# A masked-attention layer on one core: each output tile's scatter behind the next tile's adding gather, and one layernorm step moved behind the first natural tile

## The chip, the cores and the metric

The kernel runs on one core of one Trainium2 chip. The metric is the device time of one execution in microseconds (us); the kernel before takes 710.65 us, the median of 3 runs (710.3 to 715.59). The core has TensorE (PE), which multiplies; VectorE (DVE); ScalarE (ACT); GpSimd (POOL), which here mostly issues indirect DMAs; and SyncE (SP), which issues plain DMAs. Each works through its own queue in order. They meet at semaphores.

## What is computed

One layer of graph attention over 2708 nodes with 1024 features, with a layernorm ahead of it. The adjacency matrix holds a one with a chance of 0.0014771 at each place, so a node has some 4 neighbours.

```python
h = relu(layernorm(x))
q = h @ W_q.T + b_q;  k = h @ W_k.T + b_k;  v = h @ W_v.T + b_v
z = q @ k.T / sqrt(1024) * adj
z = where(z == 0, -10000, z)
x = x + relu(softmax(z, axis=1) @ v)
```

All tensors are float32.

## The kernel before

**Tiles.** The rows are cut into 22 tiles of 128 (21 full ones and a rest of 20). Since only neighbours count, no 2708 x 2708 matrix is formed. The product of the two weight matrices, M, is built first (`part_of_m`, L353, four parts on PE). Then, for every tile, q = h M + bias is formed on PE; the neighbours' rows of h are gathered one neighbour per row at a time (`gather`, L430) and multiplied with q on DVE for the scores (`scores`, L659); the weighted sum u of the same rows is formed on DVE (`sums`, L714); and u times W_v gives the output tile on PE.

**The opening.** `follow` (L239) works through strings of steps: `s14-15` loads the x rows of tiles 14 and 15 and takes their statistics on DVE (`stats`, L188), `r` takes the root of the variance on ACT and DVE (`root`, L209), `a` applies the layernorm (`apply`, L225), and `e9` loads a tile of the adjacency matrix and searches its rows for neighbours on DVE, with one pass on ACT (`edges`, L255). `apply` issues for each of its two tiles a relu on ACT (L233), a store of the rows to `h_dram` from POOL's queue (L234), and an addition into `hsum` on POOL (L235). ACT's order is that of the code here (a manual schedule); the other engines' order is set by a scheduler. After the four parts of M the first tile is turned (`turned`, L282) and multiplied (`query`, L298; L313), with the bias seeded into PSUM by ACT (L295). In the midst of that product `query` calls `open_first` for the first pair of tiles and then `follow(between[0])`. x rows lie in a ring of 7 row buffers, so that a load of later x rows or of h rows waits until an earlier holder is done with.

**Pairs of tiles.** After the first tile, tiles are taken in pairs (units). Five units hold tiles in natural order, five in an order sorted by number of neighbours (`sort`, L472, in the third unit), and ten are output units ("o"). `multiply` (L793) does a pair in seven block products instead of eight, from sums and differences of blocks (`blocks`, L518: a11, a12, a22, s1 to s4; s2 and s4 on POOL for the first units), four matmuls of 512 columns each to a block and two passes each in the profile. It calls `after(i)` between its steps. `after` moves the attention of other tiles on (`advance`, L770): gathers on POOL, scores and sums on DVE. From the sixth unit on DVE's order is that of the code too.

**The output of a tile.** In an output unit the results of a pair, ya and yb, are relued from PSUM by ACT (L866, L870, L874, L882), partly after an addition on DVE (L869, L873). L869 reads the PSUM bank into which PE adds its next block. Then POOL gathers the rows of x that belong to the tile and adds them in the DMA itself (`add_x`, L856, L859), and scatters the sum to `out` (`scatter`, L618, L619). `sent` holds the tiles whose scatter isn't issued yet; `send` issues them in `after(2)` and `after(5)`, and once behind the loop:

```python
def send(keep=0):
    while len(sent) > keep:
        y, t = sent.pop(0)
        scatter(y, t, P)
...
        def after(i):
            if i in (2, 5):
                send()
```

So ya, whose add is issued between `after(3)` and `after(4)`, is scattered at `after(5)` of the same unit, and yb at `after(2)` of the next one; each scatter waits for the landing of the add of its own tile. y tiles lie in four buffers. One tile is left over (`alone`, number 11 of the sorted order); it is done behind the loop, with its x rows gathered without an add (L1030), and so are the last 20 rows (`tail`, L895).

**The gathered rows.** 13 buffers of 0.5 MB hold gathered rows: `fill` (L644) issues a gather whenever one is free, and `sums` gives it back after its last use.

Of the kernel before, what the change touches and what calls it, by code (L numbers as in the profile page):

```python
# [15 lines left out]
ALU = mybir.AluOpType  # L16
AX = mybir.AxisListType

P = 128
# [4 lines left out]
SLOTS = 16  # L24
# [31 lines left out]
def tile_preln_masked_attention(  # L56
# [12 lines left out]
    nc = tc.nc  # L69
# [84 lines left out]
    t = 0  # L154
    while t < NT:
# [4 lines left out]
        t = e  # L160
# [7 lines left out]
    first = const.tile([P, PARTS, 8], FT, name="first")  # L168
# [70 lines left out]
    def follow(steps):  # L239

        for step in steps.split():
            if step == "a":
                apply()
            elif step == "r":
                root()
            else:

                with tc.issue_after(roots[-1].ins) if roots else nullcontext():
                    if step[0] == "s":
                        lo, hi = step[1:].split("-")  # L250
                        stats(range(int(lo), int(hi) + 1))
                    else:
                        adj_loads.append(edges(int(step[1:])))
# [44 lines left out]
    def query(hT, banks, name, first=False, between=(), mid=None):  # L298

        q = work.tile([P, D], FT, tag="q", name=f"q_{name}", bufs=4)  # L300
        order = [(h, c) for h in range(NH) for c in range(DC)]
        if first:

            order.sort(key=lambda hc: hc[1] >= DC // 2)
        def evict(h):
            nc.scalar.copy(q[:, h * NB:(h + 1) * NB], banks[h])

        for h, c in order:
            if mid is not None and (h, c) == (1, 5):
                evict(0)  # L310
                mid(mm)
                follow(between[0])
            mm = nc.tensor.matmul(banks[h], hT[:, c, :], M[:, c // 4, h, c % 4, :], start=False,  # L313
                                  stop=(c == DC - 1), skip_group_check=True)
        for h in range(NH) if mid is None else (1,):
            evict(h)
        follow(between[1])
        return q
# [4 lines left out]
    with tc.tile_pool(name="w", bufs=1, side="left") as wp:  # L323
# [74 lines left out]
        for t in range(2):  # L398
            h_e[t] = row_tile(f"h_e{t}")
            nc.sync.dma_start(h_e[t], h_dram[t * P:(t + 1) * P, :])  # L400
        follow("s14-15 e9 r e10 a")
        hT = {}

        def turn_first():
# [2 lines left out]
        banks = []  # L407
# [22 lines left out]
    def gather(dst, src, t, w, n, skip=False):  # L430
        off = bass.IndirectOffsetOnAxis(ap=ptab.bitcast(U32)[:n, t, w:w + 1], axis=0)
        if skip:
            return nc.gpsimd.indirect_dma_start(out=dst, out_offset=None, in_=src, in_offset=off,  # L433
                                                bounds_check=N - 1, oob_is_err=False)
        return nc.gpsimd.indirect_dma_start(out=dst, out_offset=None, in_=src, in_offset=off)
# [80 lines left out]
    behind = []  # L516
# [57 lines left out]
        ops_of[0][2]()  # L574
        banks_of[0] = banks_for(bp_sb)

    q = query(hT.pop(0), banks, "e0", first=True, between=('e11 s16-17', ''), mid=open_first)
    nc.scalar.dma_start(q_dram[0:P, :], q)

    steps_at = {(0, 0): 'e12 r a e13', (0, 3): 'e14 s18-19 r e15', (1, 0): 'a e16 s20-21 e17', (1, 3): 'e18 r a e19', (2, 0): 'e20 e21'}  # L580
# [37 lines left out]
    def scatter(y, t, n):  # L618
        to = nc.gpsimd.indirect_dma_start(  # L619
            out=out, out_offset=bass.IndirectOffsetOnAxis(ap=ptab.bitcast(U32)[:n, t, SLOTS:SLOTS + 1], axis=0),  # L620
            in_=y[:n], in_offset=None)
        for other in outs:
            tc.declare_no_dep(to.ins, other.ins, reason="rows of a permutation")
        outs.append(to)
# [231 lines left out]
    def add_x(y, t, n=P):  # L856

        off = bass.IndirectOffsetOnAxis(ap=ptab.bitcast(U32)[:n, t, SLOTS:SLOTS + 1], axis=0)
        nc.gpsimd.indirect_dma_start(out=y[:n], out_offset=None, in_=x, in_offset=off, compute_op=ALU.add)  # L859

    def o_results(ta, tb):
        ya = work.tile([P, D], FT, tag="q", name=f"y_{ta}", bufs=4)
        yb = work.tile([P, D], FT, tag="q", name=f"y_{tb}", bufs=4)

        def c11(X):
            nc.scalar.activation(ya[:, lo], X, AF.Relu)  # L866

        def c22(Y, p5):
            nc.vector.tensor_add(p5, Y, p5)  # L869
            nc.scalar.activation(yb[:, hi], p5, AF.Relu)  # L870

        def c12(Z, u2):
            nc.vector.tensor_add(u2, Z, u2)  # L873
            nc.scalar.activation(ya[:, hi], u2, AF.Relu)  # L874
            if ta == NT - 2:

                nc.sync.dma_start(tail_dram, ya[P - 1:, :])
            add_x(ya, ta)
            sent.append((ya, ta))

        def c21(Y):
            nc.scalar.activation(yb[:, lo], Y, AF.Relu)  # L882
            add_x(yb, tb)
            sent.append((yb, tb))

        return c11, c22, c12, c21

    sent = []

    def send(keep=0):  # L890
        while len(sent) > keep:
            y, t = sent.pop(0)
            scatter(y, t, P)

    def tail(t):  # L895
        n = tiles[t][1]
# [5 lines left out]
    def of_wv(i, j):  # L902

        return wv[j][:, i * 4:(i + 1) * 4, :]
# [4 lines left out]
    alone = order[-1]  # L909
# [30 lines left out]
    for n, unit in enumerate(units):  # L940
        kind, ta, tb = unit
        now[0] = n
        if n == FIRST:
            ordered.enter_context(tc.manual_schedule(engines={mybir.EngineType.DVE}))
        if FIRST - 1 <= n <= FIRST + 2:

            i, j = ((0, 0), (0, 1), (1, 0), (1, 1))[n - FIRST + 1]
            nc.sync.dma_start(m_dram[i, j], M[:, i, j])
        share = (20.0 if kind == "q" else 19.0) / 7
        nxt = units[n + 1] if n + 1 < len(units) else None  # L950
        results = (q_results if kind == "q" else o_results)(ta, tb)

        def after(i):
            if i in (2, 5):
                send()
            if (n, i) == (2, 3):
                with tc.issue_after(products[-1].ins):
                    placed.append(sort())
                ordered.close()
                ts_of_wv()  # L960
            if n == FIRST - 1 and i == 5:

                chain.append(behind[-1])
                next(stream)
            if n == FIRST - 1 and i == 6:
                chain.append(behind[-1])
            if (n, i) >= (FIRST, 0):
                advance(share)
            if nxt is not None:

                if i == (3 if n == FIRST - 1 else 0):
                    ops_of[n + 1] = blocks(*rows_of[n + 1], nc.gpsimd if n + 1 < FIRST - 1 else None)
                    ops_of[n + 1][1]()
                if i == (4 if n == FIRST - 1 else 2):
                    ops_of[n + 1][2]()
                    rows_of.pop(n + 1)
                    if n == last_q - 1:
                        all_rows()
                if i == 3:
                    banks_of[n + 1] = banks_for(bp_sb)  # L980
                if i == 2 and n + 2 < FIRST:
                    natural_rows(n + 2)
                if i == 4 and n + 2 >= FIRST and n + 2 < len(units) and n + 2 not in rows_of:
                    while units[n + 2][0] == "o" and not done.issuperset(units[n + 2][1:]):
                        advance(1.0)
                    rows_of[n + 2] = load_rows(units[n + 2])
            if (n, i) in steps_at:
                follow(steps_at[n, i])
            if (n, i) == (2, 1):
                searched()  # L990
            if n == last_q - 1 and i == 4:

                nc.sync.dma_start(bp_sb, bv.to_broadcast([P, D]))
                nc.vector.tensor_sub(bp_sb[:, NB:], bp_sb[:, NB:], bp_sb[:, :NB])

            for k, at in enumerate(((0, 0), (0, 1), (0, 3), (0, 4), (0, 5), (0, 6), (1, 2))):
                if (n - last_q, i) == at:
                    place, src = ((M[:, 0, 0], of_wv(0, 0)), (T[:, 0], tv_dram[0]), (T[:, 1], tv_dram[1]),
                                  (M[:, 1, 0], of_wv(1, 0)), (M[:, 1, 1], of_wv(1, 1)), (T[:, 2], tv_dram[2]),
                                  (T[:, 3], tv_dram[3]))[k]  # L1000
                    nc.sync.dma_start(place, src)

        multiply(n, results, after)
    ordered.close()
    send()
    while alone not in done:
        advance(1.0)

# [18 lines left out]
    nc.vector.tensor_copy(flag, ps_f[:, 0:1])  # L1027

    y = work.tile([P, D], FT, tag="q", name="y_alone", bufs=4)
    gather(y, x, alone, SLOTS, P)  # L1030
    tail(NT - 1)
    r, = load_rows(("o", alone))
    uT = turned(r, "alone")
# [16 lines left out]
    with tc.If(some > 0):  # L1050
        with tc.tile_pool(name="big", bufs=1, side="right") as big, tc.tile_pool(
            name="gen", bufs=1, side="right"
        ) as gen:
            hT = big.tile([P, DC, N], FT, name="hT_all")
# [17 lines left out]
            with tc.For_i(0, NT) as i:  # L1072
# [9 lines left out]
                q = gen.tile([P, D + 1], FT, tag="q", name="g_q")  # L1082
# [57 lines left out]
                y = gen.tile([P, D], FT, tag="junk", name="g_y")  # L1140
# [53 lines left out]
```

## Time and profile before

| | |
|---|---|
| median of 3 runs | 710.65 us |
| the profiled execution, its own time | 712.04 us |
| its span, first to last instruction | 710.2 us |
| mean granted clock of TensorE | 0.987 |
| gathers of neighbour rows (POOL, L433) | 106, 1199 ns each on POOL |
| adding gathers (POOL, L859) | 21, 1651 ns each on POOL |
| scatters of the output (POOL, L619) | 21, 1192 ns each on POOL |
| relus of the layernorm (ACT, L233) | 22, 1236 ns each |
| additions into hsum (POOL, L235) | 22, 2369 ns each |

The page of the profile gives for each engine its busy time and share of the span, and for groups of instructions their line, engine, operation and tiles, their number, busy time and mean. In a timeline each row is a run of like instructions: its start and length in us, engine, line, operation, output and inputs, count, and in brackets the idle time of the engine ahead of it and the instruction that ended it. In a list of waits a row names who waited, for whom, how many us in all, how often, and the longest. A float32 matmul of 512 columns stands as two passes, so a block of four as 8. Lines that begin with L are those of the kernel before.

### The profile page before, as it was taken

Reading aid. Unit: us, or ns where it says so; the run is one execution under the profiler, and the core shown is the slowest. Engines: PE = TensorE matmul, PEld = TensorE weight load, DVE = VectorE, ACT = ScalarE, POOL = GpSimd, SP = SyncE. Lnnn points to the kernel's source line nnn. Section 1 sums busy time; section 2 is a strip of 40 time slices with the busy share of each in tenths; the row PEclk is TensorE's granted clock in tenths of the full one; section 3 lists DMA queues with packets and bytes.
Section 4 is the critical chain, followed back from the end, with each engine's and each line's share of the span. In section 5 each row is a group of like instructions: output and inputs, shape, how many; then the busy total and the mean of one; then the engine's idle time right before and its main releaser. Section 6 shows DMA issues by size and latency. Waiting matters only on the chain. (4 is left out here: it accounts for less than half of the span.)

```text
span 710.2 us, 6368 instructions
## 1 busy us (share of the span) xinstructions
PE 672.7 (95%) x1796; PEld 344.8 (49%) x1796; DVE 527.5 (74%) x1053; ACT 246.6 (35%) x374; POOL 356.2 (50%) x309
## 2 busy tenths in 40 slices
PE   6999999798999999989999999999998789999995
PEld 4776776344444444434444444444443334444442
DVE  6989848969999402499897969988768768978601
ACT  0086077465853211423322204342332314313220
POOL 2057063323345565577772736365646666465333
PEclk9999999999999999999999999999999899999998
DMA  8998889999876747699986999897888678887764
GB/s 346 405 381 304 324 282 411 381 407 336 315 257 218 262 128 236 225 332 329 408 304 209 392 419 411 276 260 240 267 230 254 204 233 259 257 227 225 176 183 130
DMA packets 64164, 203.19 MB, mean 286 GB/s; under 512 B 9898, under 2 KB 10250, under 8 KB 62716
## 3 DMA queue, kind: packets, MB, share of 16 engines
q0 software_dynamic: 34448, 109.25, 47.5%
q1 hardware_dynamic: 27660, 86.67, 32.7%
q10 hardware_dynamic: 2016, 6.82, 2.5%
q8 instruction: 16, 0.26, 0.1%
q14 instruction: 24, 0.20, 0.1%
HBM read 166.62 MB, written 49.13 MB: 304 GB/s over the span
## 5 line engine op out<-in xcount | busy, mean ns | idle before, releaser
L433 POOL DMA_INDIRECT g<-h_dram,tab x106 | 127.1, 1199 | 46.8 <-issue 24.8
L781 PE MATMUL psy<-T,s 128*128 128x512 f32 x320 | 144.0, 593 | 1.8 <-ACT psy L799 1.8
L665 DVE SCALAR_TENSOR_TENSOR junk<-g,pq 128x1024 uint8<-128x1024 f32 x92 | 112.8, 1226 | 42.1 <-DMA g<-h_dram,tab 18.2
L781 PE MATMUL ps<-M,a 128*128 128x512 f32 x320 | 144.0, 592 | 0.0
L360 PE MATMUL ps_m<-wk,wq 128*128 128x512 f32 x256 | 112.7, 602 | 5.5 <-DMA wk<-in_wk_dram 5.5
L718 DVE SCALAR_TENSOR_TENSOR u<-g,coef,u 128x1024 f32<-128x1024 f32 x77 | 98.8, 1283 | 11.0 <-ACT u L710 8.5
L360 PEld LDWEIGHTS ps_m<-wk,wq 128*128 128x128 f32 x256 | 80.1, 314 | 36.2 <-DMA wk<-in_wk_dram 5.5
L781 PEld LDWEIGHTS ps<-M,a 128*128 128x128 f32 x320 | 59.6, 190 | 69.4 <-issue 69.4
L781 PEld LDWEIGHTS psy<-T,s 128*128 128x128 f32 x320 | 59.3, 190 | 69.6 <-issue 69.4
L781 PE MATMUL psy<-T,a 128*128 128x512 f32 x160 | 76.0, 620 | 13.3 <-DVE p L869 11.9
L264 DVE FIND_INDEX8 at<-ones,adj 128x8 uint32<-128x685 f32 (+1 forms) x88 | 75.3, 866 | 0.0
L781 PE MATMUL ps<-M,s 128*128 128x512 f32 x160 | 72.2, 593 | 2.2 <-ACT p L802 2.2
L781 PE MATMUL ps<-T,s 128*128 128x512 f32 x160 | 71.9, 592 | 0.0
L619 POOL DMA_INDIRECT out_dram<-y,tab x21 | 25.0, 1192 | 92.5 <-DMA y<-in_x_dram,tab 88.1
L234 POOL DMA_DIRECT2D h_dram<-x x22 | 12.2, 555 | 106.5 <-ACT x L233 106.5
L781 PEld LDWEIGHTS psy<-T,a 128*128 128x128 f32 x160 | 31.2, 199 | 54.6 <-issue 36.5
L261 ACT ACTIVATE sized<-adj 128x2708 uint8<-128x2708 f32 (+1 forms) x22 | 54.2, 2464 | 2.6 <-DMA adj<-in_adj_dram 2.5
L235 POOL TENSOR_TENSOR hsum<-hsum,x 128x1024 f32<-128x1024 f32 (+1 forms) x22 | 52.1, 2369 | 0.4
L781 PEld LDWEIGHTS ps<-M,s 128*128 128x128 f32 x160 | 30.1, 190 | 39.3 <-issue 35.9
L781 PEld LDWEIGHTS ps<-T,s 128*128 128x128 f32 x160 | 30.4, 190 | 38.3 <-issue 37.8
L710 ACT ACTIVATE u<-g,coef 128x1024 f32<-128x1024 f32 x19 | 21.9, 1151 | 47.2 <-DVE coef L709 37.2
L859 POOL DMA_INDIRECT y<-in_x_dram,tab x21 | 34.7, 1651 | 6.4 <-issue 5.2
(193 smaller groups left out, 723.6 us busy)
## 6 DMA issues: line engine op xcount, KB each, us to landing
adj<-in_adj_dram SPq DMA_DIRECT2D x21, 1354.0 KB
x<-in_x_dram SPq DMA_DIRECT2D x21, 512.0 KB
h_dram<-x POOLq DMA_DIRECT2D x21, 512.0 KB
u_dram<-u POOLq DMA_DIRECT2D x14, 512.0 KB
or<-u_dram SPq DMA_DIRECT2D x14, 512.0 KB
h_e<-h_dram SPq DMA_DIRECT2D x11, 512.0 KB
q_late<-q SPq DMA_DIRECT2D x10, 512.0 KB
pq<-q_late POOLq DMA_DIRECT2D x10, 512.0 KB
```

The lines of the kernel that those rows point to most:

```text
L234: nc.gpsimd.dma_start(h_dram[t0:t0 + n, :], xt[:n])
L235: nc.gpsimd.tensor_add(hsum[:n], hsum[:n], xt[:n])
L261: nc.scalar.activation(sized[:n], a[:n, :, :PW], AF.Abs, accum_out=total[:n, t:t + 1])
L264: nc.vector.max_index(at[:n, g, :], ones[:n, 0:8], a[:n, g, :])
L360: nc.tensor.matmul(acc[i], lhs, wk_sb[o][:, cols], start=(o == 0), stop=(o == DC - 1))
L433: return nc.gpsimd.indirect_dma_start(out=dst, out_offset=None, in_=src, in_offset=off, bounds_check=N - 1, oob_is_err=False)
L619: to = nc.gpsimd.indirect_dma_start(out=out, out_offset=bass.IndirectOffsetOnAxis(ap=ptab.bitcast(U32)[:n, t, SLOTS:SLOTS + 1], axis=0), i ...
L665: chained(lambda: nc.vector.scalar_tensor_tensor(junk, g_of[t][s], 1.0, tq[t], op0=ALU.mult, op1=ALU.mult, accum_out=zall[:, t, s:s + 1]))
L710: nc.scalar.activation(u, g_of[t][0], AF.Copy, scale=coef[:, at[t][0]:at[t][0] + 1])
L718: chained(lambda: nc.vector.scalar_tensor_tensor(u, g_of[t][s], coef[:, at[t][s]:at[t][s] + 1], u, op0=ALU.mult, op1=ALU.add))
L781: mm = nc.tensor.matmul(bank, a[:, c, :], b[:, c, :], start=False, stop=(c == 3), skip_group_check=True)
L859: nc.gpsimd.indirect_dma_start(out=y[:n], out_offset=None, in_=x, in_offset=off, compute_op=ALU.add)
```

## The change

There are two edits. In the output units a scatter is no longer issued at `after(2)` and `after(5)`; `send` now takes an instruction and is called with each adding gather: the tile that is in `sent`, which is the one before, is scattered behind that gather (`issue_after` holds the scheduler to it). For the last pair's second tile it is called with the gather of x for the lone tile. And the step `a` for tiles 14 and 15 goes from ahead of the fourth part of M into `query` of the first tile, behind `e11`.

```diff
-        follow("s14-15 e9 r e10 a")
+        follow("s14-15 e9 r e10")
...
-    q = query(hT.pop(0), banks, "e0", first=True, between=('e11 s16-17', ''), mid=open_first)
+    q = query(hT.pop(0), banks, "e0", first=True, between=('e11 a s16-17', ''), mid=open_first)
...
     def add_x(y, t, n=P):
...
-        nc.gpsimd.indirect_dma_start(out=y[:n], out_offset=None, in_=x, in_offset=off, compute_op=ALU.add)
+        return nc.gpsimd.indirect_dma_start(out=y[:n], out_offset=None, in_=x, in_offset=off, compute_op=ALU.add)
...
-            add_x(ya, ta)
+            send(add_x(ya, ta))
             sent.append((ya, ta))
...
-            add_x(yb, tb)
+            send(add_x(yb, tb))
             sent.append((yb, tb))
...
-    def send(keep=0):
-        while len(sent) > keep:
+    def send(behind):
+        while sent:
             y, t = sent.pop(0)
-            scatter(y, t, P)
+            with tc.issue_after(behind.ins):
+                scatter(y, t, P)
...
         def after(i):
-            if i in (2, 5):
-                send()
...
     ordered.close()
-    send()
...
-    gather(y, x, alone, SLOTS, P)
+    send(gather(y, x, alone, SLOTS, P))
```

In the built program the order of PE and DVE is the same as before. On ACT the two relus of tiles 14 and 15 stand behind the pass of e11. On POOL their stores and additions stand behind s2 and s4 of the first pair, and each scatter stands directly behind the add of the next tile. On SP the order of some loads between the adjacency tiles 14 and 16 and of the four stores of M to `m_dram` differs: three of those stores now stand ahead of the loads of x for tiles 16 and 17, and the loads for tiles 18 to 21 are spread between the adjacency tiles.

## The prediction

> **What bounds the kernel now.** I read, in this order: busy time by engine, what TensorE (PE) waits for, its timeline around each wait, then the timelines of VectorE (DVE), GpSimd (POOL) and ScalarE (ACT) before the wait.
>
> ```profile
> PE 672.7 (95%) x1796; PEld 344.8 (49%) x1796; DVE 527.5 (74%) x1053; ACT 246.6 (35%) x374; POOL 356.2 (50%) x309
> ```
>
> PE is busy for 95% of the span, so time can only be won where PE stands still. Its list of waits:
>
> ```profile
> PE psy L781 <- DVE p L869: 11.9, 3, 7.5
> PE ps_m L360 <- DMA wk<-in_wk_dram: 5.5, 1, 5.5
> PE ps L313 <- ACT ps L295: 3.7, 1, 3.7
> ```
>
> 11.9 us are waits for one DVE operation, L869; 5.5 us are the first weights, which the change doesn't touch; 3.7 us are a wait for ACT, once. PE's timeline at the three places (start, length, what, passes, idle before):
>
> ```profile
> 128.01 13.12 PE L313 MATMUL ps<-M,T_e 128*128 128x512 f32 x26 [3.67 <-ACT ps L295]
> ...
> 554.77 5.71 PE L781 MATMUL psy<-T,a 128*128 128x512 f32 x8 [7.54 <-DVE p L869]
> ...
> 586.61 5.15 PE L781 MATMUL psy<-T,a 128*128 128x512 f32 x8 [4.00 <-DVE p L869]
> ```
>
> A block of 8 passes takes 3.60 us everywhere else. After these stalls it takes 5.71 and 5.15, and the 26 passes take 13.12 where 26 at that pace need 11.33 (3.60 + 18 x 0.43). The granted clock is 0.83 in the slice 540 to 560, 0.91 in 580 to 600 and in 120 to 140, and 1.00 in the others around. So each stall costs its own length and 1.5 to 2.1 us behind it.
>
> Why is L869 late? DVE runs in program order, and ahead of L869 it waits for gathered rows:
>
> ```profile
> 525.80 1.23 DVE L665 SCALAR_TENSOR_TENSOR junk<-g,pq 128x1024 uint8<-128x1024 f32 x1 [2.77 <-DMA g<-h_dram,tab]
> ...
> 542.73 1.23 DVE L665 SCALAR_TENSOR_TENSOR junk<-g,pq 128x1024 uint8<-128x1024 f32 x1 [2.97 <-DMA g<-h_dram,tab]
> ...
> 554.03 0.69 DVE L869 TENSOR_TENSOR p<-psy,p 128x512 f32<-128x512 f32 x1
> ```
>
> From 511 to 554 there are six such waits: 2.26, 2.36, 0.76, 2.77, 2.97, 0.15, together 11.27 us. From 555 to 586 another 2.51 + 1.65 + 3.82 = 7.98. And POOL, which issues the gathers, stands still at the same time:
>
> ```profile
> POOL out_dram L619 <- DMA y<-in_x_dram,tab: 88.1, 20, 9.8
> ```
>
> ```profile
> 515.05 1.59 POOL L859 DMA_INDIRECT y<-in_x_dram,tab  x1 [0.30 <-issue]
> 516.95 1.01 POOL L433 DMA_INDIRECT g<-h_dram,tab  x1 [0.30 <-issue]
> 518.27 1.32 POOL L433 DMA_INDIRECT g<-h_dram,tab  x1 [0.30 <-issue]
> 525.22 0.99 POOL L619 DMA_INDIRECT out_dram<-y,tab  x1 [5.63 <-DMA y<-in_x_dram,tab]
> ```
>
> The scatter (L619) waits for the adding gather (L859) of the same tile, 4.4 us on the mean of 20, and the gathers of g queue behind it. They waited for little else: with DVE and its buffers they have "0.30 issue" nearly everywhere.
>
> **The scatter moved behind the next tile's add.** Nothing is added or removed: 21 adds, 21 scatters, the same bytes. In the built order each scatter stands directly behind the add of the next tile. An add takes from its start to its landing (where the scatter's wait ends) 6.5 to 11.4 us over the 16 adds up to 660. Those adds start 11.3 to 18.6 us apart, and the relus that they follow end 8.7 to 22 us apart, so the tile in between covers the wait: I take 0 for it, and up to 2.7 us for the odd pair (11.4 - 8.7). What took its place could be the add itself, which waits for ACT's relu. Today POOL reaches an add 4.8 to 15.9 us after its relu is done, 10 to 16 us from 461 to 572. So POOL can catch up by about that much before the add becomes the wait; behind the add stand the gathers of DVE's later work. The gathers can also become bound by their 13 buffers; from free buffer to use there are several operations of 1.3 us, against an issue of 1.2 us and a landing, so a small residue is left.
>
> The first stall needs DVE 7.54 us earlier and has 11.27 us of waits to lose. At the second PE comes 7.54 + 2.11 = 9.65 us earlier and wants no wait of 4.00, so DVE must be 13.6 us earlier; it has 11.27 + 7.98 = 19.2. So the stalls go if 70% of the waits go. Then 7.54 + (5.71 - 3.60) + 4.00 + (5.15 - 3.60) = 15.2 us are won. What is late next: with PE 15.2 us ahead, DVE's later L869s and the lone last tile. Its sum ends at 665.1, its row is stored at 668.9 and PE turns it at 683.4; some 11 us earlier is needed there, and by then DVE has 25 us of waits to lose (7.98 and 11.27, and 1.71, 0.31, 3.82 up to 640). DVE's own work from 511 to 665 is then about 129 us beside 139 of PE: it fits, but not by much. I leave 1.5 us of stall standing, about half a wait of today's: 13.7 us won, between 4.8 (three quarters of the waits stay, so DVE is 11.27 / 4 = 2.8 earlier at the first stall and 19.2 / 4 = 4.8 at the second) and 15.2. At the end nothing hangs on the scatters: the last one follows PE's end by DVE's last operation, as now.
>
> **The layernorm of tiles 14 and 15 moved.** On ACT two relus of 1.19 us leave the place ahead of the first tile's turning, and with them ACT's wait for their root.
>
> ```profile
> 123.15 2.38 ACT L233 ACTIVATE x<-x,r 128x1024 f32<-128x1024 f32 x2 [2.51 <-DVE r L221]
> ...
> 127.34 1.13 ACT L295 COPY ps<-bp_sb 128x512 f32<-128x512 f32 x2
> ```
>
> ACT is free at 120.6; M's products end on PE at 123.5 and its turning of the second tile at 124.3. The seeds of L295 then come at about 123.3, so PE doesn't wait: 3.67 and 13.12 - 11.33 = 1.79 go, 5.46 us. Most of it is given back. The next block, ps<-T,s at 147.85, would be reached at 142.4, but needs s1 from DVE (L529, at 145.40), and DVE has been in one piece since 125.4. It gets something back:
>
> ```profile
> 128.88 1.66 DVE L266 TENSOR_TENSOR cand<-first,at 128x32 f32<-128x32 f32 x1
> ```
>
> This small subtraction takes 0.19 elsewhere; here POOL's add of x15 into hsum (128.12 to 130.48) runs beside it. Without the add it wins 1.47, so s1 is there at 144.6 and PE starts at 144.7: 3.15 us won, a new stall of 2.3. Does that slow the clock? The rows show no loss after 1.57 us and 1.8 after 3.67. The Trainium skill ("TensorE: Matmul & The Clock Gate", Why this matters for your kernels) puts the limit at idle gaps of about 3 us. By the rule the stall is free, by the worse row it costs 1.8; I take 0.
>
> Then comes a chain on ACT: copies of the next turning, e12's pass (2.6), root, two relus of tiles 16 and 17 (2.4), e13's pass (2.6), and p5, for which PE waits 1.36 at 162.30. It starts 3.15 earlier. But POOL's moved adds, now behind s2 and s4, fall on 148.5 to 153.7, and DVE's six root operations on about 152.5. The Trainium skill ("GPSIMD Engine Reference", Key points) speaks against the change here: POOL shares its SBUF interfaces with DVE and hinders instructions with two SBUF inputs. Taken for the whole of both adds that would be 4.7 us; the rows have 1.21 for L218 at 196.44 (0.16 alone), and 1.66 to 2.47 for L266 and L267. I take 1.2: p5, and with it PE and DVE's search, are 3.15 - 1.2 = 2.0 us earlier (between 3.2 with no hold and -1 with a hold over more than one add). The two relus on ACT now stand before the psy copy at 148.05; it ends near 146.5 and PE wants it at 149.0, so 2.5 us cover them.
>
> Two stores of 0.5 MB (0.56 us on POOL) move too. On SP a load that waited 8.0 us for x14's store now waits for PE at 124.3, so tiles 16 and 17 are asked for at about 128, not 136.6; but x19 and x21 now wait for the stores of x14 and x15 (issued near 148 and 151, landing some 7 us later as at 124.69 to 131.9), and adj 15 is queued behind x19. I get 156.8 for it, 155.5 now; DVE searches it near 170, so 13 us cover a load of 1.35 MB. If that cover went, every us would go into the sort and all gathers.
>
> **Sum.** 13.7 + 2.0 = 15.7 us from the profiled execution (712.04, span 710.2, the rest lies around it) gives 696.3. The profiled time is 1.4 above the median of the runs, 710.65; from that, 695.0.
>
> **Rivals.** (1) Three quarters of the gathers' waits stay, bound by buffers or by adds that wait for relu. For: 13 buffers, and one tile of 15 rows fills them. Against: POOL was nearly never held by DVE. Then 4.8 + 2.0 are won: 703.8. (2) The moved layernorm wins nothing or costs 1: the DVE hold or adj 15. For: DMA is at 0.9 to 1.0 from 100 to 180. Then 697 to 698. (3) Slower: POOL's queue locks step with PE. An add that waits for its relu blocks the gathers that DVE needs before its next PSUM operation, so PE's own lateness comes back. It decides when the adds wait more than the 4.4 us that the scatters wait today; at 7 us each POOL loses 140 us for 88, and at today's rate (15.2 of PE for 88) PE loses 9 more: 718. Against: 20 us of DVE work lie between the L873 at 511 and the use of the first gather behind its add. That the change doesn't do what it says is excluded by the built order.
>
> **How the numbers follow.** Forecast 0.60 (692 to 699 its own range); rival 2, 0.13; rival 1, 0.17; rival 3 and the like, 0.10. Faster by over 1% (about what a measurement can tell from no change) means under 703.5: 0.60 + 0.13 + a third of rival 1, 0.79; the rest of rival 1 is within 1%, with a little of rival 3: 0.13; slower 0.08. The range starts at 15.2 + 3.2 us and one small stall more, 691, and reaches to rival 1, 704.
>
> **What would show it.** Right: L619 waits for its add a few us in total, not 88; PE's waits for L869 under 3 us; no block of 5 us; the first L313 without wait, and a wait of about 2 us ahead of ps<-T,s near 145. Wrong: L859 waiting for ACT, g waiting for DVE, DVE still waiting for g between 500 and 600, or adj late near 170.

## The result, and the profile after

| | before | after |
|---|---|---|
| median us | 712.77 (710.3 to 715.59, 4 runs) | 693.37 (692.02 to 695.18, 4 runs) |
| the profiled execution, its own time | 712.04 | 695.18 |
| its span | 710.2 | 693.4 |
| mean granted clock of TensorE | 0.987 | 0.996 |
| GpSimd: scatter waits for the add of its own tile | 88.1 us, 20 times | 2.9 us, 2 times |
| GpSimd: add waits for ScalarE's relu | 0.6 us, 2 times | 35.6 us, 9 times |

The changed kernel is faster: ratio 0.9728, 95% interval 0.9676 to 0.978. The forecast was 695.0 us (range 691 to 704). The kernel before has four runs here; the 710.65 us that the forecast starts from was the median of three of them. The two profiled executions differ by 16.9 us in time and 16.8 in span; the forecast's sum was 15.7.

The busy times of the engines after, from the head of the page:

```profile
PE 668.1 (96%) x1796; PEld 343.3 (50%) x1796; DVE 526.4 (76%) x1053; ACT 246.8 (36%) x374; POOL 364.9 (53%) x309
```

PE's busy time fell by 4.6 us although it does the same 1796 instructions. The three pieces that ran slower behind a stall are 5.5 us shorter in all (L313 14.1 us for 15.9, `psy<-T,a` 72.3 for 76.0); the four parts of M took 1.2 us longer in this execution (113.9 for 112.7), lost in the first 30 us, ahead of both changes. The other 12 us are stalls. What PE waits for (us in all, times, longest):

```profile
PE ps_m L360 <- DMA wk<-in_wk_dram: 5.6, 1, 5.6
PE psy L781 <- DVE q L841: 2.6, 2, 1.4
PE ps L781 <- DVE s L529: 2.4, 1, 2.4
PE ps L781 <- ACT p L802: 2.2, 2, 1.4
```

The waits for L869 (11.9 us) and for L295 (3.7) are gone. In their place stand the wait for s1 that was forecast (L529), and the wait for L841 in the first units, 2.6 us for 1.4 before (0.53 and 0.91). PE's timeline at the places to compare:

```profile
124.84 11.32 PE L313 MATMUL ps<-M,T_e 128*128 128x512 f32 x26
...
145.40 3.67 PE L781 MATMUL ps<-T,s 128*128 128x512 f32 x8 [2.35 <-DVE s L529]
...
159.98 3.67 PE L781 MATMUL ps<-M,s 128*128 128x512 f32 x8 [1.41 <-ACT p L802]
...
315.40 1.06 PE L279 MATMUL pt<-ident,qr 128*128 128x128 f32 x8 [1.73 <-DMA qr<-h_dram,tab]
...
546.28 3.70 PE L781 MATMUL psy<-T,a 128*128 128x512 f32 x8
```

The 26 passes take 11.32, not 13.12, and start without a wait. The row at 315.40 is the last stall of the run: from 320 to the end of PE's work at 684.85 PE stands still for 0.12 us in all. Why, is read on DVE. Of waits for gathered rows there is none left behind 425, and DVE now waits for PE at several places:

```profile
509.89 0.69 DVE L873 TENSOR_TENSOR u<-ps,u 128x512 f32<-128x512 f32 x1 [1.61 <-PE ps L781]
...
545.55 0.68 DVE L869 TENSOR_TENSOR p<-psy,p 128x512 f32<-128x512 f32 x1
```

At the place of the first stall there is no room to spare: DVE works without a pause from 535.67 to the end of L869 at 546.23, and PE's block, which stood for 7.54 us before, starts directly behind it, at 546.28, with 0.12 us lost. At the next two such blocks (571.95 and 597.73) L869 is done 2.0 and 1.8 us ahead.

And on GpSimd, first its waits, then the place that the prediction showed at 515 and the end of its queue:

```profile
POOL out_dram L619 <- DMA y<-in_x_dram,tab: 2.9, 2, 1.8
POOL y L859 <- ACT y L874: 19.2, 5, 8.2
POOL y L859 <- ACT y L882: 16.4, 4, 7.8
POOL y L859 <- DMA tail_dram<-y: 10.3, 1, 10.3
```

```profile
511.51 1.64 POOL L859 DMA_INDIRECT y<-in_x_dram,tab  x1 [4.78 <-ACT y L874]
513.46 1.01 POOL L619 DMA_INDIRECT out_dram<-y,tab  x1 [0.31 <-issue]
...
623.31 1.00 POOL L433 DMA_INDIRECT g<-h_dram,tab  x1 [0.31 <-issue]
628.02 2.16 POOL L859 DMA_INDIRECT y<-in_x_dram,tab  x1 [3.71 <-ACT y L882]
...
664.93 1.55 POOL L859 DMA_INDIRECT y<-in_x_dram,tab  x1 [8.21 <-ACT y L874]
```

The scatter follows the add of the next tile with nothing between, and doesn't wait: the add of its own tile was started at 498.92, 14.5 us ahead. GpSimd's queue has caught up so far that the add now waits for the relu. The long ones of these waits come at the end. The row at 623.31 is the last gather of neighbour rows. Ahead of it adds wait for relus five times, 12.9 us in all, 4.78 at most. The other four waits, 22.6 us, and one of 10.3 for a small store of a row of the add's tile, which follows the relu, lie behind it, where no such gather stands in the queue any more.

### The profile page after: what moved, and what is told of

Its sections match the earlier page's. It is cut to its first block, busy times and chain, and to the rows that moved or that the text cites. A ratio compares the mean times of both kernels' runs of the same rounds, so it can differ in the third digit from the quotient of the medians.

```text
span 693.4 us, 6371 instructions
## 1 busy us (share of the span) xinstructions
PE 668.1 (96%) x1796; PEld 343.3 (50%) x1796; DVE 526.4 (76%) x1053; ACT 246.8 (36%) x374; POOL 364.9 (53%) x309
## 5 line engine op out<-in xcount | busy, mean ns | idle before, releaser
L433 POOL DMA_INDIRECT g<-h_dram,tab x106 | 132.0, 1246 | 51.5 <-issue 22.1
L781 PE MATMUL psy<-T,s 128*128 128x512 f32 x320 | 144.1, 593 | 1.8 <-ACT psy L799 1.8
L781 PE MATMUL ps<-M,a 128*128 128x512 f32 x320 | 144.1, 592 | 0.0
L665 DVE SCALAR_TENSOR_TENSOR junk<-g,pq 128x1024 uint8<-128x1024 f32 x92 | 112.6, 1224 | 16.9 <-DMA pq<-q_dram,tab 14.7
L360 PE MATMUL ps_m<-wk,wq 128*128 128x512 f32 x256 | 113.9, 607 | 5.6 <-DMA wk<-in_wk_dram 5.6
L781 PEld LDWEIGHTS ps<-M,a 128*128 128x128 f32 x320 | 59.7, 190 | 69.3 <-issue 69.3
L781 PEld LDWEIGHTS psy<-T,s 128*128 128x128 f32 x320 | 59.4, 190 | 69.6 <-issue 69.6
L781 PE MATMUL psy<-T,a 128*128 128x512 f32 x160 | 72.3, 595 | 2.7 <-DVE q L841 2.6
L781 PE MATMUL ps<-M,s 128*128 128x512 f32 x160 | 72.2, 593 | 2.2 <-ACT p L802 2.2
L781 PE MATMUL ps<-T,s 128*128 128x512 f32 x160 | 72.0, 593 | 2.4 <-DVE s L529 2.4
L859 POOL DMA_INDIRECT y<-in_x_dram,tab x21 | 39.3, 1870 | 49.7 <-ACT y L874 19.2
L781 PEld LDWEIGHTS ps<-T,s 128*128 128x128 f32 x160 | 30.4, 190 | 40.9 <-issue 37.8
L781 PEld LDWEIGHTS psy<-T,a 128*128 128x128 f32 x160 | 30.0, 190 | 41.2 <-issue 34.9
L781 PEld LDWEIGHTS ps<-M,s 128*128 128x128 f32 x160 | 30.1, 190 | 39.3 <-issue 36.1
L525 ACT COPY a<-pt 128x512 f32<-128x512 f32 x60 | 33.5, 595 | 8.4 <-PE pt L279 8.4
## 6 DMA issues: line engine op xcount, KB each, us to landing
h_e<-h_dram SPq DMA_DIRECT2D x11, 512.0 KB, 10.3
```

Of the source, the lines that this page charges most:

```text
L360: nc.tensor.matmul(acc[i], lhs, wk_sb[o][:, cols], start=(o == 0), stop=(o == DC - 1))
L525: nc.scalar.copy(ops[name], bank)
L665: chained(lambda: nc.vector.scalar_tensor_tensor(junk, g_of[t][s], 1.0, tq[t], op0=ALU.mult, op1=ALU.mult, accum_out=zall[:, t, s:s + 1]))
L781: mm = nc.tensor.matmul(bank, a[:, c, :], b[:, c, :], start=False, stop=(c == 3), skip_group_check=True)
L859: return nc.gpsimd.indirect_dma_start(out=y[:n], out_offset=None, in_=x, in_offset=off, compute_op=ALU.add)
```

## The experiments

The theory: the scatter edit makes nearly all of the gain, because GpSimd's queue no longer stands for landings, DVE gets its rows early and PE its PSUM banks; the layernorm edit wins a few us in the opening, most of which come back in later waits. The main rival: the two parts share the gain, or the queue's order matters and not the wait. Ratios are to the kernel before on the same chip, with a 95% interval.

### One part alone

`p1_scatter` undoes the second edit:

```diff
-        follow("s14-15 e9 r e10")
+        follow("s14-15 e9 r e10 a")
...
-    q = query(hT.pop(0), banks, "e0", first=True, between=('e11 a s16-17', ''), mid=open_first)
+    q = query(hT.pop(0), banks, "e0", first=True, between=('e11 s16-17', ''), mid=open_first)
```

> The scatter moved alone; the layernorm of tiles 14 and 15 stays where it was. Theory (POOL standing still for the scatters makes the gathers late, DVE behind them, and so PE's two stalls): nearly the whole gain stays. PE has no wait for L869, no block of over 5 us after 500, and the wait of 3.67 us ahead of the first L313 is back with its slowed passes. Against the changed kernel it is 1 to 2 us longer, so a span near 695. Rival (the layernorm made the room): under half of the 16.8 us of span stays, 702 or more.

Measured: 695.65 us, ratio 0.9764 (0.972 to 0.9807). PE's wait for the seeds is back, with its slowed passes, and no stall is left behind 316:

```profile
127.31 13.12 PE L313 MATMUL ps<-M,T_e 128*128 128x512 f32 x26 [3.22 <-ACT ps L295]
```

`p2_layernorm` is the kernel before with the second edit alone.

> The layernorm moved alone; the scatters stay as before. Theory: PE is 2.5 to 3 us earlier near 145 and 1 us earlier near 316, but the stalls at 547 and 583 are set by DVE waiting for gathers, so only what reaches POOL's chain of gathers is kept: 0 to 2 us less than before, span 708.5 to 710.5. Rival (it gains by itself what was forecast): 2.0 us in every place to the end, and the first L313 without its wait. Rival (it costs): adj 15 late, over 711.

Measured: 710.29 us, ratio 0.9983 (0.9952 to 1.0014): not to be told from no change. Its trace shows the won stall and what it turned into:

```profile
145.07 5.37 PE L781 MATMUL ps<-T,s 128*128 128x512 f32 x8 [2.35 <-DVE s L529]
...
555.71 5.45 PE L781 MATMUL psy<-T,a 128*128 128x512 f32 x8 [9.12 <-DVE p L869]
...
585.03 3.70 PE L781 MATMUL psy<-T,a 128*128 128x512 f32 x8 [1.74 <-DVE p L869]
```

PE waits as long for s1 as in the changed kernel, 2.35 us, but the block behind it takes 5.37 us instead of 3.67. At 555 PE arrives 0.6 us earlier than before (546.6 for 547.2) and yet goes on 0.9 us later: L869 is behind DVE's waits for rows, GpSimd's queue still stands 81.9 us for landings, and the stall has grown from 7.54 to 9.12. So what PE had won in the opening is gone at this place, where DVE isn't earlier. At the next stall DVE is earlier, because a gather of q rows kept it waiting 1.15 us and not 3.82; PE waits 1.74 us there and not 4.00, and the span of this one execution is 2.7 us shorter than before. No link from the moved layernorm to that gather is shown, and over twelve runs no gain can be told.

From the ratios the scatter part alone is 0.0236 x 712 = 16.8 us (13.7 to 19.9) and the layernorm part alone 0.0017 x 712 = 1.2 us (-1.0 to 3.4). Together 18.0, and the whole change is 0.0272 x 712.77 = 19.4 (15.7 to 23.1): the parts add up within what is measured. That the layernorm part alone gains anything is not shown by the runs; its interval takes in 0.

### Where the scatter stands

`two_behind` keeps one more tile back, so that a scatter comes behind the second next add:

```diff
-    def send(behind):
-        while sent:
+    def send(behind, keep=1):
+        while len(sent) > keep:
...
-    send(gather(y, x, alone, SLOTS, P))
+    send(gather(y, x, alone, SLOTS, P), 0)
```

> The changed kernel with each scatter one tile later still: behind the second next add. Theory: the wait is already 0 at one tile, so nothing more is won: span within 1 us of 693.4, provided the four y buffers are free in time (a y is rewritten two units later, so they are). Rival (distance itself helps the DMA queue): 2 us or more faster. Rival (buffers): ACT's relus wait for a scatter, and it is slower.

Measured: 698.69 us, ratio 0.9801 (0.9748 to 0.9855). PE has no stall behind 315 here either, and ends at 684.08, 0.8 us earlier than in the changed kernel. The 3.3 us of longer span lie behind PE's end, on GpSimd:

```profile
671.52 1.00 POOL L435 DMA_INDIRECT y_alone<-in_x_dram,tab  x1 [4.51 <-DMA out_dram<-y,tab]
...
681.59 1.43 POOL L619 DMA_INDIRECT out_dram<-y,tab  x1 [4.61 <-DMA y<-in_x_dram,tab]
...
689.13 0.99 POOL L619 DMA_INDIRECT out_dram<-y_alone,tab  x1 [0.30 <-issue]
```

y tiles have four buffers. With one more tile held back, the lone tile's gather waits for a scatter to give its buffer up, the last scatters bunch up, and the final one is issued at 689.13 where the changed kernel issues it at 685.87. So one tile of distance is enough to hide the landing, and a second one costs a buffer at the end. Both the theory (within 1 us of the changed kernel) and its proviso on the buffers were wrong there: the rival that named the buffers had the right place, though the one that waits is the lone tile's gather and not a relu.

`own_add` puts the scatter behind the add of its own tile:

```diff
-            send(add_x(ya, ta))
             sent.append((ya, ta))
+            send(add_x(ya, ta))
...
-            send(add_x(yb, tb))
             sent.append((yb, tb))
+            send(add_x(yb, tb))
...
-    send(gather(y, x, alone, SLOTS, P))
+    gather(y, x, alone, SLOTS, P)
```

> The changed kernel with each scatter directly behind the add of its own tile, no gather in between; everything else equal. Theory: the wait of a scatter is an add's issue to landing less its own time on POOL, 5 to 9 us, so POOL stands some 130 us for the scatters where the kernel before stands 88. DVE waits for g again and PE for L869; at the rate of before (15.6 us of PE for 88 us) 23 us are lost to the changed kernel: span near 716, between 709 and 728. Rival (what helps is only that scatters no longer mix with adds and gathers in the DMA queue): about as before with the layernorm moved, 709, or less.

Measured: 712.04 us, ratio 0.9998 (0.9966 to 1.003). The gain is gone and PE's stalls for L869 are back, with their slowed blocks:

```profile
551.57 5.21 PE L781 MATMUL psy<-T,a 128*128 128x512 f32 x8 [5.75 <-DVE p L869]
...
581.24 5.40 PE L781 MATMUL psy<-T,a 128*128 128x512 f32 x8 [2.33 <-DVE p L869]
```

The size was missed: I had counted on 130 us of standing, but

```profile
POOL out_dram L619 <- DMA y<-in_x_dram,tab: 91.6, 20, 10.0
```

The reason is in the built order. "Behind" is all that the edit asks for, and the scheduler still set one to three gathers or loads between most adds and their scatters, as in the kernel before. From the start of the add to the start of the scatter there are 7.8 us on the mean in both. So this run is close to the kernel before with the layernorm edit (`p2_layernorm`), in its built order as in its time, and tells that the place of the scatter decides. Its own rival, that a scatter merely shouldn't mix with adds and gathers in the queue, isn't tested by it, since they still mix. What the scatter costs directly behind its add is left to the next run.

`own_direct` is `own_add` with the gathers of neighbour rows and the loads of pq held behind that scatter:

```diff
-            with tc.issue_after(first_q[0].ins) if first_q else nullcontext():
+            with tc.issue_after((outs or first_q)[-1].ins) if first_q else nullcontext():
                 gather(g, h_dram[:, :], t, s, P, skip=True)
...
-            nc.gpsimd.dma_start(tq[t], q_late[...])
+            with tc.issue_after((outs or first_q)[-1].ins):
+                nc.gpsimd.dma_start(tq[t], q_late[...])
```

> The changed kernel with each scatter directly behind the add of its own tile, and the gathers and loads of pq of later tiles held behind that scatter (in own_add, one to three of them still stood between, as in the kernel before, and the time was the kernel before's). Theory (the wait is the add's landing, 7.8 us from the add's start on the mean in both traces, less what is issued in between): GpSimd stands 20 x (7.8 - 1.65 - 0.3), about 115 us, against 91.6, so some 25 more; TensorE's waits for L869 grow by the same share as in the kernel before (15.2 of 88), 4 us: about 716 (711 to 724). Rival (the landing is earlier when no gather stands behind the add in the queue, so that the wait is the same): 88 to 95 us of standing and 710 to 713.

Measured: 774.43 us, ratio 1.0838 (1.0791 to 1.0885). Both theories missed it by some 60 us. The scatters' own waits are 97.4 us, hardly more than 91.6. What is new is that the scheduler can no longer place a later tile's gather ahead of an add that waits for ACT: the adds now wait 59.7 us in all for relus and the tail's store, where in `own_add` they waited 0.6. A stretch of GpSimd's timeline in this kernel, and PE's longest stall (L860 and L782 are the L859 and L781 of the others):

```profile
601.74 1.89 POOL L860 DMA_INDIRECT y<-in_x_dram,tab  x1 [7.86 <-ACT w L682]
608.40 1.01 POOL L619 DMA_INDIRECT out_dram<-y,tab  x1 [4.78 <-DMA y<-in_x_dram,tab]
...
629.38 1.68 POOL L860 DMA_INDIRECT y<-in_x_dram,tab  x1 [12.86 <-ACT y L875]
```

```profile
623.66 6.57 PE L782 MATMUL ps<-T,s 128*128 128x512 f32 x8 [16.99 <-DVE s L529]
```

The add waits 7.86 us for ACT, its scatter 4.78, then come the gathers (610 to 615), DVE has waited 11.24 us for one of them, s1 of the next pair is late behind it, PE stands 16.99 us, and so the next relu and the next add are late: 12.86. This is the lockstep of rival 3, in a kernel that forces it. The run changes two things, the scatter's place and the gathers' order, and doesn't divide the 80 us between them; that the scatters' waits grew by only 6, and the adds' by 59, speaks for the order. So the half of the main rival that names the queue's order is right as far as order can cost a great deal. It doesn't take the wait's place in the account of the gain: `two_behind`, another order without the wait, leaves PE without stalls, and `own_add`, close to the old order and with the wait, has them.

### What is left in the opening

The stall of 2.35 us for s1 and the 1.41 us for p5 could be worth some 3 us more. `s1_first` moves one subtraction of DVE (L428, 2.29 us), which stood ahead of s1 and is needed only later:

```diff
-    ts_of_m(0, 1, 2, 3)
+    ts_of_m(0, 1, 2)
...
         ops_of[0][2]()
+        with tc.issue_after(behind[1].ins):
+            ts_of_m(3)
         banks_of[0] = banks_for(bp_sb)
```

> The changed kernel with one operation of VectorE moved: the fourth subtraction for T (L428, 2.29 us) stands behind s1 and s3 instead of ahead of them, so s1 is there about 2.2 us earlier. Nothing is added or removed. Theory (the new stall ahead of ps<-T,s is VectorE's order alone, and what TensorE wins in the opening is carried to the end): the stall of 2.35 us at 145.4 is under 0.4, ps<-T,s starts at about 143.1, the span is 1.5 to 2.3 shorter than the changed kernel's: 691.1 to 691.9 us against 693.4. Rival (VectorE's search and the sort set when TensorE may go on near 316, so the opening's gains fade there, as 3.0 us at 160 became 1.7 at 316): the stall goes too, but the waits at 310 and 315 grow by as much, and the time stays within 0.5 us of the changed kernel's.

`e13_later` moves a pass of ACT from ahead of p5 to behind it:

```diff
-    steps_at = {(0, 0): 'e12 r a e13', (0, 3): 'e14 s18-19 r e15', ...
+    steps_at = {(0, 0): 'e12 r a', (0, 1): 'e13', (0, 3): 'e14 s18-19 r e15', ...
```

> The changed kernel with the step e13 (a pass of ScalarE, 2.6 us, and a search on VectorE) one place later, so that p5 stands ahead of its pass; with it eight transposes on TensorE and one load of h rows on SyncE come later. Theory (TensorE's own waits are what counts): the wait of 1.41 us ahead of ps<-M,s at 160 goes and the time is 1.0 to 1.4 us shorter than the changed kernel's: about 692.2. Rival (VectorE, in one piece from 154 to 220 with searches, sets the time near 316): the wait goes, TensorE is early at 160 and 208, the waits at 310 and 315 grow, and the time is the changed kernel's within 0.5 us.

With them ran the changed kernel again.

> The changed kernel once more, unedited, beside the next kernels on the same chip, so that differences of one or two us can be read against it. Both theories: ratio to the kernel before 0.973 +- 0.004, about 693.4 us.

Measured: `after_again` 694.23 us, ratio 0.9722 (0.9694 to 0.9751); `s1_first` 692.58, ratio 0.9706 (0.968 to 0.9733); `e13_later` 696.42, ratio 0.9754 (0.9726 to 0.9782). In `s1_first` the stall for s1 is gone, and in its profile the next one has grown (L783 and L804 are the L781 and L802 of the others):

```profile
160.99 6.72 PE L783 MATMUL ps<-M,s 128*128 128x512 f32 x8 [3.38 <-ACT p L804]
```

Its cause is a row of DVE and two of GpSimd:

```profile
152.54 2.19 DVE L217 SCALAR_TENSOR_TENSOR r<-mv,r 128x2 f32<-128x2 f32 x1
```

```profile
145.73 3.21 POOL L529 TENSOR_TENSOR s<-a,s 128x512 f32<-128x512 f32 x1
...
152.34 2.37 POOL L235 TENSOR_TENSOR hsum<-hsum,x 128x1024 f32<-128x1024 f32 x1
```

The root's small operation takes 0.23 us in the changed kernel; here it starts 0.2 us behind the second of the moved additions and stands until that is done (154.73 and 154.71). The relus behind the root come that much later, and p5 behind them. The edit has a hand in it: the moved subtraction now runs beside s4 on GpSimd, which takes 3.21 us for 1.27 in the changed kernel, and the additions behind s4 come that much later, onto the root. In `e13_later` the wait for p5 goes, but PE then waits 2.98 us for DVE's L841, where the changed kernel waits 1.18, and the block behind takes 5.40 us:

```profile
176.58 5.40 PE L781 MATMUL psy<-T,a 128*128 128x512 f32 x8 [2.98 <-DVE q L841]
```

DVE works in one piece there and comes to L841 at 175.85, not earlier than in the changed kernel (174.39). Neither of its two theories had that: the time was to be 1 us shorter or the same, and is 2.2 us longer, with intervals that still overlap.

Since the median and the profile of `s1_first` disagreed, it ran again, with the changed kernel and with both edits together (`s1_e13`).

> The changed kernel unedited, as the mate of the next two on the same chip: 693 to 694.5 us, ratio to the kernel before 0.972 +- 0.003 (693.37 and 694.23 so far).

> The same kernel as s1_first, whose median was 1.65 us below the changed kernel's while its profiled execution showed the won 2.35 us of stall coming back in the wait for p5 (3.38 for 1.41), behind a root operation of VectorE that GpSimd's addition held for 2.19 us. If the median is the truth (part of the stall is carried to the end), the difference to the changed kernel is 1 to 2 us again; if the profile is (the gain turns into the next wait), it is under 0.5.

> Both edits of the opening together: the fourth subtraction for T behind s1 and s3, and e13 one place later. Alone, the first turned its gain into the wait for p5, the second turned its gain into a wait of 2.98 us for VectorE's L841 at 176. Theory (VectorE, in one piece from 154 to 176, sets when TensorE goes on near 176): p5's wait goes, the wait for L841 is 3 to 5 us, and the time is not below the changed kernel's: 693.5 to 697. Rival (the two waits were each other's and both go): 690 to 691.5.

Measured: `after_third` 693.71 us, ratio 0.9728 (0.9695 to 0.976); `s1_first_twin` 693.94, ratio 0.9738 (0.9708 to 0.9769); `s1_e13` 695.14, ratio 0.9765 (0.9734 to 0.9796). So the profile was right: the gain of `s1_first` turns into the next wait (3.35 us for p5 in the twin as well; the rival had looked for it at 310 and 315), the difference of the first medians wasn't confirmed, and with both edits PE waits 1.78 us for p5 and 2.99 for L841. None of the three beats the changed kernel.

## Why the prediction was right, step by step

**The scatter part was right, and somewhat undervalued.** The summed stalls and slowed blocks of the profiled executions: 7.54 + 2.11, 4.00 + 1.55 and small ones of 0.4, some 15.6 us, against 13.7 forecast; `p1_scatter` alone gives 16.8 (13.7 to 19.9). The term that failed is "I leave 1.5 us of stall standing": nothing stayed. "It fits, but not by much" was exact at 546, where PE's block starts directly behind L869, and too careful elsewhere, where DVE waits for PE. That no stall is left at 546 is a near thing, then, and it is the same in `p1_scatter` and `two_behind`, where PE's block also starts 0.05 us behind the end of L869. Of the 25 us of waits that were to be lost, 8.0 were for rows of q and not for gathered rows of h; they went too. That the tile in between covers the landing is shown by 2.9 us of waits for 21 scatters, both at the very end (the last pair's second tile and the last 20 rows), and by `two_behind`, where more distance wins nothing.

**What took the wait's place** is what was named: adds that wait for relus, 35.6 us in nine waits of up to 8.2. Rival 3 was to decide when an add waits more than the 4.4 us that a scatter waited. On the mean of all 21 adds it is 1.7 us, or 2.2 with the tail's store, and 0.9 for the 15 adds up to the last gather; so rival 3 wasn't reached, and that the waits of 8 us cost PE nothing proves little, since no gather stood behind them. Its price, though, was worked out on the wrong quantity. It counted 9 us of PE for 52 more of POOL's waits. In `own_direct` the adds wait 2.8 us on the mean, under the limit of 4.4, POOL's waits for both are 157 us in all, 68 more than before, and the time is 61 us longer than before. So the sum of the waits doesn't decide; what decides, as far as this run shows it, is whether the gathers that DVE needs next have been issued ahead of the waiting add.

**The layernorm part** was right in its early terms but one. The stall at L313 and its 1.8 us of slowed passes went, s1 made PE wait 2.35 (forecast 2.3, at 144.7; the trace has 145.40), and L266 takes 0.19 for 1.66. The hold of the root by hsum, put at 1.2 us, was 0.07 in the changed kernel, since the second addition ended at 153.69, 0.2 us after L217 had started. That was luck: `s1_first`, where L217 starts 0.2 us behind the addition's start, shows a price of 2.0. The stall of 2.35 was costed at no slowed passes. That holds in the profiled execution, but not in general: in five of eight traces with this stall the block behind it took 5.35 to 5.37 us, 1.7 more. Where it does, the won 5.46 leave about 5.46 - 2.35 - 1.7 = 1.4 us at this place. `p2_layernorm`, with 1.2 (-1.0 to 3.4), neither confirms that nor speaks against it.

**The gain in the opening fades.** Counted from the turning of the first h rows, which lies ahead of both edits (112.61 after, 111.94 before), PE is 3.1 us ahead at 145, 3.0 at 160, 2.4 at 208 and 1.7 at 316. The forecast had 2.0 us at 160 and carried them to the end; for a fading it had no term. The load of adjacency tile 15 was to be issued at 156.8 with 13 us of cover; it was issued at 156.68, and DVE waited 0.54 us for it at 169.97, so in this execution the cover was just used up (the two other traces of the changed kernel have no such wait):

```profile
169.97 0.09 DVE L264 MATCH_VALUE_LOAD at<-ones,adj 128x8 f32 x1 [0.54 <-DMA adj<-in_adj_dram]
```

That DVE's searches set this stretch is what `e13_later` and `s1_e13` show: PE, earlier at 160 (159.69 and 156.27, for 159.98), waits longer for L841 (2.98 and 2.99, for 1.18).

**The sum.** 15.6 + 1.07 (PE's last stall of the opening at 315.40 for 316.47) is 16.7 of the 16.8 us of span. The forecast, 13.7 + 2.0, had the first term 1.9 us too low and the second 0.9 too high, so that a part of the errors cancelled. The medians fell by more, 712.77 to 693.37, for two reasons: the profiled execution after, 695.18, is the slowest of its four; and the kernel before had medians of 712.1 to 713.7 beside all the later runs, not the 710.65 that the forecast subtracted from. The forecast's ratio, 695.0 / 710.65 = 0.978, is the end of the measured interval.

## What to carry to other kernels

On an in-order queue that feeds another engine, put between a transfer and its dependent one as much other work as the landing takes, by handing the dependent one on to the next round; then check that the operation which now waits isn't ahead of what the fed engine needs next. Look for the built order, not for the order asked for: "behind" leaves the scheduler free to place other work between, for good or ill. A stall removed early in a kernel counts only as far as the next engine down the line gets earlier as well.

## What the runs showed of the hardware

- How a stall slows what follows varies from one execution to another and doesn't grow with its length. The changed kernel, stalled 2.35, 2.76 and 2.04 us at the same place in three executions, took 3.67, 5.37 and 5.37 us for the next block of 8 passes. In the 13 traces, 16 stalls of 2.04 to 3.55 us stand ahead of such a block: 11 were followed by a slowed one (5.35 to 6.72 us), five were not (2.35 twice, 2.49, and 3.35 and 3.54 in `own_direct`). All eight stalls from 4.00 to 16.99 us were, with 5.15 to 6.57 us. The Trainium skill ("TensorE: Matmul & The Clock Gate", Why this matters for your kernels) puts the limit at about 3 us of idling; these traces have losses of 1.7 us from 2.04 on, and none behind 3.54.
- A DVE operation of 256 elements in and out (L217) takes 0.16 us alone and 2.17 to 2.19 beside a GpSimd addition of 128x1024 that starts just before it, and 0.23 when it starts 0.2 us before the addition ends. In these rows it is held for the remainder of the addition, not slowed by a share. The reciprocal ahead of it (L216, one input) ran beside the same addition in the changed kernel and kept its 0.17 us.
